# Neighbour counts in two levels, a sort that looks one round ahead, and one addition moved to VectorE in a four-layer graph kernel

## The chip, the cores and the metric

The kernel runs on one core of a Trainium2 chip. The metric is the device time of one execution in microseconds (us): the median of three runs before the change is 5041.57 us (5023.24 to 5044.63). TensorE is called PE, VectorE DVE, ScalarE ACT and GpSimd POOL, as in the profile; SP is the queue that issues plain transfers.

## What is computed

There are 16 independent graphs ("entries") of N = 1024 nodes with C = 64 features. Four layers follow one another, each as `x = layernorm(x + layer(x))`. Layers 0 and 1 multiply the dense 1024 x 1024 adjacency matrix by the features. Layers 2 and 3 first thin out each node's neighbours and then aggregate quantiles over what is left:

```python
nb = (adj_ > 0) & (~eye)
m = nb.sum(-1)
rank = cumsum(nb, axis=-1) - 1
skip = where(m > 10, (m + 1) // 2, 1)
removed = nb & (skip > 1) & mask & ((rank + 1) % skip == 0)
rem = removed | swapaxes(removed, 1, 2)
valid = where(rem, 0, adj_) > 0
# per node and feature: sort the features of the valid neighbours,
# 0.25*q(0.25) + 0.5*q(0.5) + 0.25*q(0.75), interpolated
h = relu((x + agg) @ W1 + b1);  y = h @ W2 + b2
```

With these inputs a node has at most some 33 slots (its own and its neighbours).

## The kernel before

**Tiles and rounds.** The nodes of an entry are ordered by their number of neighbours, so that 128 nodes of like degree stand in one tile. Seven tiles of an entry (10 to 19 slots, `SIZES[:7]`) are filled by POOL: an indirect DMA per slot gathers 128 rows of 64 features from a table in memory (`fetch`, into the ring `got_s` of `ROOM = 60` slots). The eighth tile holds the nodes with the most neighbours; the halves of two entries' eighth tiles are put together to two "end blocks" of 21 and 33 slots (`got`). These are not gathered but picked: VectorE or ScalarE makes a one-hot tile (`hot`) from the slot numbers `place`, and PE multiplies it by the features, split in three bf16 parts (`pick`, 24 matmuls a slot, into `pgk`); ScalarE copies the result out of PSUM (`empty` in `fill`). Only one pair of end blocks is in memory, so that the picks of a round begin when the 33-slot block of the round before is used up.

A round is one layer (2 or 3) of one pair of entries: 8 pairs times 2 layers give 16 rounds. In a round VectorE sorts each tile by a network of min and max operations on slots (`exchange`); ScalarE then multiplies the slots that quantiles need by weights, and PE adds them up by matmuls with an identity (`weigh`); an MLP and a layer norm follow (`finish_round`). In round 0 the two entries' tiles are sorted one by one, later both at once.

**The stages before a round.** For each entry `features` computes layers 0 and 1, `cuts` finds where neighbours are removed, `lists` builds the index lists (takes, pv, keys, order, pk, best, idx) and `ordered` the tables and `place`. `cuts` needs the running count of neighbours up to each column. For each of the eight column tiles t and each half h of 512 columns it adds up, over all row tiles c that come before or within the half, `near` (0 or 1, the stationary operand) times a slice of `steps`, a matrix of ones and zeros with a step: 4 + 8 matmuls of 512 columns a tile, 96 an entry, into `pr`. ScalarE passes over each `pr` twice (Sign with a sum, written to `junk`); the sums tell the columns at which neighbours are cut.

**What sets the order.** Nothing is scheduled by hand, and nothing is decided on the chip. While the program is built, a planner with clocks of its own (`Clocks`, `Weave`) runs all stages as generators, and each instruction is issued when the planner believes that its operands are ready. The order so found is fixed in each engine's queue (VectorE, ScalarE and PE are scheduled by the planner). On the chip each engine takes its instructions in this order and waits where the planner was wrong.

`sorting` calls `sort_round(k)` for one round after the other: it opens `fill(k)`, takes the ring's tiles of this round as they arrive, and an end block when it is filled (an end block that is ready goes ahead of a tile that is ready). When the tiles of the round are done and an end block is not filled, it yields until it is. `allowed[0] = k + 4` lets the stages of later entries begin when round k begins.

In the profile nearly all lines are L300, that of the helper which records each instruction; the tiles' names tell them apart.

Of the kernel before, what the change touches and what calls it, by code (L numbers as in the profile page):

```python
# [22 lines left out]
P = 128  # L23
# [301 lines left out]
def adj_resnorm_kernel(ctx: ExitStack, tc: tile.TileContext, x, adj_t, nodemask, w01, b01, w02, b02,  # L325
# [33 lines left out]

    ONSET = HALF - P  # L360
    steps = const.tile([P, ONSET + N], BF, name="steps")
    row_id = const.tile([P, NT], F32, name="row_id")
    nc.gpsimd.iota(row_id, pattern=[[P, NT]], base=0, channel_multiplier=1,
                   allow_small_or_imprecise_dtypes=True)
# [281 lines left out]
    def cuts(b, e):  # L646

        while e.near is None or (b and not entries[b - 1].taken):
            yield
        near = e.near  # L650

        e.st = st = s.work.tile([P, 6, NT], F32, name="nb_st", bufs=2)
        half = s.work.tile([P, NT], I32, name="nb_half", bufs=1)
        m, dil, lim, cut_at = st[:, 0], st[:, 1], st[:, 2:4], st[:, 4:6]
        mask = mask_all[:, b, :]
        bank, pm = yield from big("pm")
        for t in range(NT):
            for c in range(NT):
                nc.tensor.matmul(pm[:, t : t + 1], near[:, c, t * P : (t + 1) * P], one, start=c == 0, stop=c == NT - 1)
        yield  # L660
        nc.scalar.copy(m, pm[:, :NT])
        read_big[bank] = True
        yield
        dve.tensor_scalar(dil, m, T_THRESH, None, op0=ALU.is_gt)
        dve.tensor_mul(dil, dil, mask)
        dve.tensor_scalar(half, m, 1.0, None, op0=ALU.add)
        dve.tensor_scalar(half, half, 1, None, op0=ALU.logical_shift_right)
        dve.tensor_copy(m, half)
        for i in range(2):
            dve.tensor_scalar(lim[:, i], m, float(i + 1), -NEVER, op0=ALU.mult, op1=ALU.add)  # L670
            dve.tensor_mul(lim[:, i], lim[:, i], dil)
            dve.tensor_scalar(lim[:, i], lim[:, i], NEVER - 0.5, None, op0=ALU.add)
        prs = []
        for t in range(NT + 1):
            if t:
                bank, pr = prs[t - 1]
                for i in range(2):
                    nc.scalar.activation(no_output([P, N]), pr, AF.Sign, bias=lim[:, i, t - 1 : t], scale=-1.0,
                                         accum_out=cut_at[:, i, t - 1 : t], saturate=False)
                read_big[bank] = True  # L680
            if t < NT:
                bank, pr = yield from big("pr")
                prs.append((bank, pr))
                for h in range(NH):
# [12 lines left out]
        e.cut = True  # L697

    def lists(b, e):
# [75 lines left out]
        minus_at = s.work.tile([1, N], F16, name="minus_at", bufs=1)  # L775
# [276 lines left out]
    def weigh(k, t, got, agg, which, present):  # L1052

        want = wants[t]
        while any(e.wts is None for m, b, e in members(k)[1] if m in present):
            yield
        if t >= LISTED:
            wts = members(k)[1][0][2].ends
            for i, slot_id in enumerate(want):
                nc.scalar.activation(got[:, i, :], got[:, slot_id, :], AF.Copy, scale=wts[:, t - LISTED, i : i + 1])  # L1060
                if i % 12 == 11:
                    yield
        else:
            for i, slot_id in enumerate(want):
                for m, b, e in members(k)[1]:
                    if m in present:
                        nc.scalar.activation(got[:, m, i, :], got[:, m, slot_id, :], AF.Copy,
                                             scale=e.wts[:, t, i : i + 1])
                if i % 6 == 5:
                    yield  # L1070
        yield
        prods = got[:, None, : len(want)] if t >= LISTED else got[:, which, : len(want)]
        left = len(want)
        for _ in range(HALVINGS):
            more = left // 2
            dve.tensor_add(prods[:, :, :more], prods[:, :, :more], prods[:, :, left - more : left])
            left -= more
        if HALVINGS:
            yield
        while adding:  # L1080
            yield
        adding.add(k)
        layer, both = members(k)
        for m, b, e in both:
            if m not in present:
                continue
            rows, at = slice(0, P), min(t, NT - 1)
            if t >= LISTED:
                rows, prods = (lower, upper)[halves_of(m).index(t)], got
            else:  # L1090
                prods = got[:, m]
            own = slice(m * C, (m + 1) * C)
            for i in range(left):
                nc.tensor.matmul(acc[own, rows], prods[:, i, :], ident[:, rows], start=i == 0, stop=False)
            nc.tensor.matmul(acc[own, rows], e.xs[layer][:, at, :], ident[:, rows], start=False, stop=True)
        free.add((k, t, present))
        free.add((k, t))
        yield
        if t >= LISTED:
            for m in range(2):  # L1100
                own, rows = slice(m * C, (m + 1) * C), (lower, upper)[halves_of(m).index(t)]
                nc.scalar.copy(agg[own, at, rows], acc[own, rows])
        else:
            own = slice(present[0] * C, (present[-1] + 1) * C)
            nc.scalar.copy(agg[own, at, :], acc[own])
        adding.remove(k)
# [186 lines left out]
    def sort_round(k):  # L1293

        if k >= 2:
            while weave.runs(rounds[k - 2]):
                yield
        weave.add(fill(k))
        agg = s.feat.tile([2 * C, NT, P], F32, name="agg")
        sums = []  # L1300
        todo = [n for n in range(len(tasks)) if tasks[n][0] == k]
        ends = [NS - 2, NS - 1]
        while todo or ends:
            options = []
            if todo and all(fetched[m] > todo[0] for m in tasks[todo[0]][2]):
                got, present = gots[todo[0]], tasks[todo[0]][2]
                options.append((max(clocks.now, clocks.when(got[:, present[0] : present[-1] + 1])), 1, todo[0]))
            if ends and (k, (1, SIZES[NS - 2])[ends[0] - NS + 2]) in filled:
                options.append((max(clocks.now, clocks.when(tails[k][ends[0] - LISTED])), 0, ends[0]))
            if not options:  # L1310
                yield
                continue
            at, is_tile, n = min(options)
# [6 lines left out]
            if is_tile:  # L1320
                _, t, present = tasks[n]
                todo.pop(0)
                got, which, count = gots[n], slice(present[0], present[-1] + 1), len(present)
                other = other[:, : count * SIZES[t], :].rearrange("p (e s) c -> p e s c", e=count)
                yield from exchange(t, (got[:, which], other), cut_pair)
            else:
                t, got, which, present = n, tails[k][n - LISTED], None, (0, 1)
                ends.pop(0)
                yield from exchange(t, (got, other[:, : SIZES[t], :]), cut)
            sums.append(weave.add(weigh(k, t, got, agg, which, present)))  # L1330
        if k:
            while weave.runs(rounds[k - 1]):
                yield
        rounds.append(weave.add(finish_round(k, agg, sums)))

    def sorting():

        for k in range(len(order_of_rounds)):
            allowed[0] = k + 4
            yield from sort_round(k)  # L1340

    with ExitStack() as main:

# [307 lines left out]
```

## Time and profile before

| what | us |
|---|---|
| median of three runs | 5041.57 |
| the profiled execution | 5036.86 |
| its span, first to last instruction | 5035.1 |
| first gather starts / last gather ends | 179.4 / 4961 |
| mean granted clock of PE | 0.85 of full |
| picks: `pgk<-x0p,hot` and `pgk<-x1p,hot`, 24576 matmuls, busy | 976.7 |
| slot weights on ScalarE, `got_s<-got_s,wts`, busy | 398.9 |
| Sign passes `junk<-pr`, 256 of 1111 ns, busy | 284.3 |
| `minus_at<-at_row`, 16 copies of 1 x 1024 on ScalarE, mean | 1.01 |

A group's busy time is what its instructions took together, and the idle time behind the bar is that of the engine just before them, with what ended it. Neighbouring matmuls overlap, so that their spacing is less than their duration. Of pr 1448 of 1536 matmuls are in the trace. Round k's gathers are the k-th 184 in order (2944 in all): those of round 4 begin at 1540 us, those of round 9 at 2963 us, those of round 15 at 4684 us.

### The profile page before, as it was taken

The numbers are of one execution on the slowest core, as the hardware profiler recorded it, in microseconds if no ns is written. First come the engines' busy times: TensorE is split into PE (matmuls) and PEld (weight loads), VectorE is DVE, ScalarE is ACT, GpSimd is POOL, SyncE is SP. The second block draws the span as 40 slices with busy tenths as digits, with TensorE's granted clock in tenths as the row PEclk, the third lists the DMA queues.
The fourth block names the chain that finished last, engine by engine and source line by source line (L and its number), as shares of the span: only waits on it lengthen the run. The fifth ranks groups of instructions, "written<-read, shape, count | busy, mean of one in ns | idle before, by whom it ended". The sixth has DMA issues, their size and how long they took to land. (4 is left out here: it accounts for less than half of the span.)

```text
span 5035.1 us, 123964 instructions
## 1 busy us (share of the span) xinstructions
PE 3791.2 (75%) x50028; PEld 3000.9 (60%) x50200; DVE 4018.0 (80%) x8678; ACT 3079.9 (61%) x7175; POOL 3312.4 (66%) x3168
## 2 busy tenths in 40 slices
PE   6887988887888787888788777888878675563532
PEld 5565666757675665666567575666666554453431
DVE  2568558897898978888888987988798888879593
ACT  4667666657677766667676676666766664452422
POOL 0436217776377775777667675777757776777774
PEclk9989987898999888889899888888988887776765
DMA  3222222322221221222222231222212111111110
GB/s 89 66 68 59 59 65 63 79 58 57 55 67 38 60 64 37 53 68 59 49 55 63 47 72 38 44 68 55 64 46 51 23 30 23 25 30 23 26 24 16
DMA packets 416740, 256.08 MB, mean 51 GB/s; under 512 B 104586, under 2 KB 367002, under 8 KB 416154
## 3 DMA queue, kind: packets, MB, share of 16 engines
q0 software_dynamic: 98304, 100.86, 11.2%
q1 hardware_dynamic: 317850, 147.19, 10.2%
q8 instruction: 395, 6.47, 0.6%
q14 instruction: 191, 1.56, 0.1%
HBM read 235.24 MB, written 12.59 MB: 49 GB/s over the span
## 5 line engine op out<-in xcount | busy, mean ns | idle before, releaser
L300 POOL DMA_INDIRECT got_s<-table,idx x2944 | 3165.2, 1075 | 1629.4 <-issue 509.9
L300 PEld LDWEIGHTS <-hot 128*128 128x128 bf16 x24576 | 902.5, 106 | 457.8 <-issue 265.7
L300 DVE TENSOR_TENSOR other<-got_s 128x512 f32<-128x512 f32 (+9 forms) x850 | 507.0, 609 | 114.6 <-DMA got_s<-table,idx 97.0
L300 PE MATMUL pgk<-x1p,hot 128*128 128x64 bf16 x12288 | 488.7, 205 | 142.0 <-ACT got L300 76.0
L300 PE MATMUL pgk<-ident,got_s 128*64 128x128 f32 x3136 | 423.5, 311 | 226.8 <-ACT got_s L300 177.3
L300 ACT ACTIVATE got_s<-got_s,wts 128x64 f32<-128x64 f32 x1568 | 398.9, 335 | 312.0 <-DVE got_s L300 307.3
L300 PE MATMUL pgk<-x0p,hot 128*128 128x64 bf16 x12288 | 488.0, 204 | 111.9 <-ACT got L300 75.8
L300 PEld LDWEIGHTS pgk<-ident,got_s 128*64 128x64 f32 x3136 | 377.4, 156 | 262.5 <-ACT got_s L300 197.0
L300 PEld LDWEIGHTS <-order 128*128 128x128 bf16 x6912 | 349.2, 100 | 258.6 <-issue 96.4
L300 PEld LDWEIGHTS <-near 128*128 128x128 fp8e4 x4608 | 343.9, 101 | 212.6 <-issue 59.4
L300 DVE TENSOR_SCALAR hot<-place 128x1024 bf16<-128x1024 f16 x768 | 304.1, 437 | 207.3 <-PE pgk L300 195.1
L300 PE MATMUL pk<-near,order 128*128 128x512 fp8e4 x1792 | 438.7, 389 | 0.0
L300 ACT COPY got<-pgk 64x192 f32<-64x192 f32 (+1 forms) x576 | 175.0, 304 | 379.1 <-PE pgk L300 372.6
L300 DVE TENSOR_TENSOR got_s<-other 128x512 f32<-128x512 f32 (+9 forms) x731 | 400.6, 563 | 7.8
L300 DVE TENSOR_TENSOR got_s<-got_s 128x512 f32<-128x512 f32 (+10 forms) x629 | 371.8, 595 | 16.2
L300 PE MATMUL pr<-steps,near 128*128 128x512 bf16 x1448 | 350.9, 386 | 21.3 <-ACT code L300 10.6
L300 ACT ACTIVATE code<-pk,ends_of 128x1024 f16<-128x1024 f32 x224 | 240.0, 1105 | 200.5 <-DVE best L300 101.5
L300 DVE TENSOR_TENSOR other<-other 128x384 f32<-128x384 f32 (+10 forms) x617 | 324.0, 525 | 18.6
L300 ACT ACTIVATE junk<-pr,nb_st 128x1024 fp8e4<-128x1024 f32 x256 | 284.3, 1111 | 62.9 <-PE pr L300 57.3
L300 ACT ACTIVATE hot<-place,minus_k 128x1024 bf16<-128x1024 f16 x256 | 292.7, 1143 | 42.6 <-PE pgk L300 36.4
L300 DVE MAX8 best<-code 128x8 f16<-128x1024 f16 x240 | 283.2, 1216 | 30.1 <-ACT code L300 29.2
L300 ACT ACTIVATE hot<-hot,one_f 128x1024 bf16<-128x1024 bf16 x256 | 294.0, 1148 | 8.4
(200 smaller groups left out, 7122.0 us busy)
## 6 DMA issues: line engine op xcount, KB each, us to landing
adj_r<-in_adj_dram SPq DMA_DIRECT2D x256, 512.0 KB
got_s<-table,idx POOLq DMA_INDIRECT x2944
x_s<-in_x_dram SPq DMA_DIRECT2D x16, 256.0 KB
table<-x2s SPq DMA_DIRECT2D x16, 256.0 KB
table<-xn SPq DMA_DIRECT2D x16, 256.0 KB
out_dram<-xn,out_rows POOLq DMA_INDIRECT x128
table<-no_row SPq DMA_DIRECT2D x12, 0.2 KB
w21s<-in_L_gnn_W_dram SPq DMA_DIRECT2D x2, 32.0 KB
```

Source lines behind the costliest of these rows:

```text
L300: return call(*args, **kwargs)
```

## The change

There are three parts.

1. Counts in two levels. A new constant `after` (zeros, then ones) gives, by 14 matmuls of 512 columns an entry, the number of neighbours in all row tiles before each row tile: `before`, 8 x 1024. ScalarE copies it to `ahead`. Then each half of `pr` begins with one matmul of 512 columns that spreads these eight numbers over the row tiles' columns (by a slice of the identity, broadcast), and each row tile adds its own running count by one matmul of 128 columns. `minus_at`, which `lists` uses, lives in the same constant tile `aside` as `ahead`, in other partitions.
2. `sort_round` and `sorting` become one generator that can have two rounds open. When a round has no ring tiles left, the next is opened (its `fill` queued, its stages allowed), and its tiles are sorted if no end block of the present round is ready. A ready end block still goes first, then tiles of the present round, then those of the next. End blocks of the next round wait.
3. In `weigh`, for rounds 0 and 1, the weighted slots are added in pairs once on VectorE, so that PE has about half of them to add. Before, `HALVINGS = 0` left this out in all rounds.

```diff
+    after = const.tile([P, 2 * NT - 1], BF, name="after")
+    nc.vector.memset(after[:, :NT], 0.0)
+    nc.vector.memset(after[:, NT:], 1.0)
+    aside = const.tile([P // 4 + NT, N], F16, name="aside")
+    minus_at, ahead = aside[:1], aside[P // 4 :]
...
+        bank, po = yield from big("before")
+        blocks = slice(P // 4, P // 4 + NT)
+        for h in range(NH):
+            wide = slice(h * HALF, (h + 1) * HALF)
+            for c in range(NT - 1):
+                nc.tensor.matmul(po[blocks, wide], after[:, NT - 1 - c :][:, :NT], near[:, c, wide], start=c == 0,
+                                 stop=c == NT - 2)
+        yield
+        nc.scalar.copy(ahead, po[blocks])
+        read_big[bank] = True
+        yield
...
                 for h in range(NH):
-                    cs = range((h + 1) * HALF // P)
-                    for c in cs:
-                        nc.tensor.matmul(pr[:, h * HALF : (h + 1) * HALF], near[:, c, t * P : (t + 1) * P],
-                                         steps[:, ONSET + h * HALF - c * P :][:, :HALF], start=c == 0, stop=c == cs[-1])
+                    own = ident_b[blocks, P // 4 + h * G :][:, :G]
+                    nc.tensor.matmul(pr[:, h * HALF : (h + 1) * HALF], ahead[:, rows],
+                                     own[:, :, None].to_broadcast([NT, G, P]), start=True, stop=False)
+                    for c in range(h * G, (h + 1) * G):
+                        nc.tensor.matmul(pr[:, c * P : (c + 1) * P], near[:, c, rows], steps[:, ONSET : ONSET + P],
+                                         start=False, stop=c == (h + 1) * G - 1)
...
-        for _ in range(HALVINGS):
+        for _ in range(1 if k < 2 else 0):
             more = left // 2
             dve.tensor_add(prods[:, :, :more], prods[:, :, :more], prods[:, :, left - more : left])
             left -= more
-        if HALVINGS:
+        if k < 2:
             yield
...
+        while True:
+            if not begun or (len(begun) == 1 and not begun[0].todo):
+                k = begun[-1].k + 1 if begun else len(rounds)
+                if k <= last and (k < 2 or (len(rounds) > k - 2 and not weave.runs(rounds[k - 2]))):
+                    allowed[0] = k + 4
+                    begun.append(open_round(k))
             options = []
-            if todo and all(fetched[m] > todo[0] for m in tasks[todo[0]][2]):
...
+            for later, r in enumerate(begun):
+                if r.todo and all(fetched[m] > r.todo[0] for m in tasks[r.todo[0]][2]):
+                    got, present = gots[r.todo[0]], tasks[r.todo[0]][2]
+                    options.append((max(clocks.now, clocks.when(got[:, present[0] : present[-1] + 1])), 2 * later + 1, r.todo[0], r))
+                if r.ends and not later and (r.k, (1, SIZES[NS - 2])[r.ends[0] - NS + 2]) in filled:
+                    options.append((max(clocks.now, clocks.when(tails[r.k][r.ends[0] - LISTED])), 0, r.ends[0], r))
...
+            if not r.todo and not r.ends:
+                begun.remove(r)
+                while rounds and weave.runs(rounds[-1]):
+                    yield
+                rounds.append(weave.add(finish_round(r.k, r.agg, r.sums)))
+                if r.k == last:
+                    return
```

More of the change, by code (lines that the diff above doesn't have):

```diff
@@ L683, in cuts @@
                 prs.append((bank, pr))
+                rows = slice(t * P, (t + 1) * P)
                 for h in range(NH):
-                    cs = range((h + 1) * HALF // P)
-                    for c in cs:
-                        nc.tensor.matmul(pr[:, h * HALF : (h + 1) * HALF], near[:, c, t * P : (t + 1) * P],
-                                         steps[:, ONSET + h * HALF - c * P :][:, :HALF], start=c == 0, stop=c == cs[-1])
+                    own = ident_b[blocks, P // 4 + h * G :][:, :G]
[4 more added lines that the diff above has]
+                                         start=False, stop=c == (h + 1) * G - 1)
             yield
@@ L774, in lists @@
         yield
-        minus_at = s.work.tile([1, N], F16, name="minus_at", bufs=1)
         nc.scalar.activation(minus_at, pn[:1], AF.Copy, scale=-0.5 / N)
@@ L1291, in exchange, with open_round, sorting @@
             yield clocks.now
[L1293 to L1297, printed above, removed]
+    def open_round(k):
         weave.add(fill(k))
         agg = s.feat.tile([2 * C, NT, P], F32, name="agg")
[L1300 to L1303, printed above, removed]
-            options = []
-            if todo and all(fetched[m] > todo[0] for m in tasks[todo[0]][2]):
[L1306 to L1309, printed above, removed]
+        return SimpleNamespace(k=k, agg=agg, sums=[], todo=[n for n in range(len(tasks)) if tasks[n][0] == k],
+                               ends=[NS - 2, NS - 1])
+    def sorting():
+        last = len(order_of_rounds) - 1
+        begun, sums = [], []
+        while True:
[4 more added lines that the diff above has]
+                    begun.append(open_round(k))
+            options = []
+            for later, r in enumerate(begun):
[4 more added lines that the diff above has]
+                    options.append((max(clocks.now, clocks.when(tails[r.k][r.ends[0] - LISTED])), 0, r.ends[0], r))
             if not options:
@@ L1312, in sort_round @@
                 continue
[L1313 removed]
+            at, rank, n, r = min(options, key=lambda o: o[:3])
             if at > clocks.now:
@@ L1319, in sort_round @@
             other = s.lists.tile([P, WIDE, C], F32, name="other", bufs=1)
-            if is_tile:
+            if rank:
                 _, t, present = tasks[n]
-                todo.pop(0)
+                r.todo.pop(0)
                 got, which, count = gots[n], slice(present[0], present[-1] + 1), len(present)
@@ L1326, in sort_round @@
             else:
-                t, got, which, present = n, tails[k][n - LISTED], None, (0, 1)
-                ends.pop(0)
+                t, got, which, present = n, tails[r.k][n - LISTED], None, (0, 1)
+                r.ends.pop(0)
                 yield from exchange(t, (got, other[:, : SIZES[t], :]), cut)
[L1330 to L1340, printed above, removed]
+            sums.append(weave.add(weigh(r.k, t, got, r.agg, which, present)))
+            r.sums.append(sums[-1])
+            if not r.todo and not r.ends:
[5 more added lines that the diff above has]
+                    return
     with ExitStack() as main:
```

## The prediction

> **What bounds the kernel now.** I read the page's busy line and slices first, then the gathers of POOL in order of time, then the places where POOL stands still, and last the engines in those places.
>
> ```profile
> PE 3791.2 (75%) x50028; PEld 3000.9 (60%) x50200; DVE 4018.0 (80%) x8678; ACT 3079.9 (61%) x7175; POOL 3312.4 (66%) x3168
> ...
> DVE  2568558897898978888888987988798888879593
> ...
> POOL 0436217776377775777667675777757776777774
> ```
>
> No engine is full, so a chain of hand-overs sets the time. POOL is nearer its limit than 66% says. It issues 2944 gathers, and between two that follow at once stand 0.30 us; the group of gathers, by shape, has 1075 ns each:
>
> ```profile
> L300 POOL DMA_INDIRECT got_s<-table,idx x2944 | 3165.2, 1075 | 1629.4 <-issue 509.9 <-DMA got_s<-table,idx 219.7 <-DVE other L300 179.8
> L300 PE MATMUL pr<-steps,near 128*128 128x512 bf16 x1448 | 350.9, 386 | 21.3 <-ACT code L300 10.6 <-ACT junk L300 5.0 <-issue 1.4
> ```
>
> So 2944 x 1.375 = 4048 us of the 5035.1 us span is gathering. The first gather starts at 179 us, the last ends at 4961 us, and 74 us follow. Real standstills of POOL (over 1 us) between these two sum to 569 us in its timeline. Up to 1341 us they are 351 us, mostly waits for an entry's index list or table; after it they are 218 us, about one a round: the ring of 60 slots is full because the sort on VectorE is behind. One of each kind, from the timeline of POOL:
>
> ```profile
> 580.25 0.97 POOL L300 DMA_INDIRECT got_s<-table,idx  x1 [91.82 <-DMA table<-x2s]
> ...
> 739.56 0.94 POOL L300 DMA_INDIRECT got_s<-table,idx  x1 [99.65 <-DVE idx L300]
> ...
> 3127.44 1.84 POOL L300 DMA_INDIRECT got_s<-table,idx  x1 [34.12 <-DVE own L300]
> ...
> 3705.33 1.67 POOL L300 DMA_INDIRECT got_s<-table,idx  x1 [46.24 <-DVE other L300]
> ```
>
> Those 569 us are the ceiling of any gain that leaves the gathers alone. In rounds 3 to 11 VectorE is what fills the ring: it is busy 2386 of the 2780 us from 1340 to 4120. Where does it idle? Between a round's two end blocks. These are four such stretches (rounds 7, 8, 10, 11: from the last operation on the 21-slot block to the first on the 33-slot block), in the table of busy times by stretch, columns PE, weight load, DVE, ACT, POOL:
>
> ```profile
> 2748.30:2776.80 28.50, 24.43 (x403) 16.90 (x405) 3.31 (x12) 19.74 (x40) 21.57 (x23) 1.00 0.15 28
> 3042.30:3065.40 23.10, 22.06 (x360) 16.45 (x362) 3.44 (x7) 13.55 (x31) 17.51 (x18) 1.00 0.15 27
> 3619.50:3643.50 24.00, 23.28 (x386) 17.40 (x390) 5.74 (x12) 17.20 (x38) 18.21 (x20) 1.00 0.20 38
> 3914.50:3936.20 21.70, 20.18 (x303) 13.65 (x306) 2.02 (x4) 15.83 (x35) 16.52 (x18) 1.00 0.17 29
> ```
>
> VectorE works 14.5 of 97.3 us, PE 90. In PE's timeline of the first stretch the picks that fill the end block share PE with the neighbour counts (pr) of a later entry:
>
> ```profile
> 2758.26 2.75 PE L300 MATMUL pr<-steps,near 128*128 128x512 bf16 x11
> ...
> 2762.01 0.87 PE L300 MATMUL pgk<-x0p,hot 128*128 128x64 bf16 x24
> 2762.72 2.75 PE L300 MATMUL pr<-steps,near 128*128 128x512 bf16 x11
> ...
> 2769.51 2.75 PE L300 MATMUL pr<-steps,near 128*128 128x512 bf16 x11
> ```
>
> Four pr blocks, some 10.5 us, lie in those 28.5 us. So between the end blocks PE is the bound, VectorE waits for it with the next round's tiles already gathered, and POOL pays when the ring fills.
>
> **What the Trainium skill says.** "Perfetto Trace Analysis", section "Identifying the Most-Contended Engine": busy time of matmuls is no good measure of PE. The trace agrees: a pr matmul lasts 386 ns, yet the next starts 216 ns later (median). I cost PE by start-to-start spacing. "TensorE: Matmul & The Clock Gate", section "Back-to-back issue gap": N/2.4 + 2.5 ns when warm, 216 ns at 512 columns and 56 at 128, but about 81 ns at 128 columns with a weight load each. Here 128-column matmuls with a load each (there_o) start 56 ns apart, so I use 56. "Perfetto Trace Analysis", section "Identifying Performance Opportunities" ("Consistent bubbles"): a gap that repeats can mean too little room for the next tile; POOL's one gap a round is that. "TensorE: Matmul & The Clock Gate", section "Architectural detail": PE may pull weight loads forward, matmuls stay in order. No run here tests it, but it is why a matmul that waits for ScalarE holds up the picks behind it.
>
> **Counts in two levels.** For an entry, 96 pr matmuls of 512 columns go: 96 x 0.216 = 20.7 us. In come 14 matmuls of 512 columns (before; near as moving operand, which in pk also has 216 ns): 3.0 us; 16 of 512 columns from the copied counts: 3.5 us; 64 of 128 columns at 0.056: 3.6 us. Together 10.1 us, so 10.6 us an entry and 170 us of PE in 16 entries. A pr block of one t falls from 12 x 0.216 = 2.6 to 2 x 0.216 + 8 x 0.056 = 0.9 us. ScalarE gets 16 copies of 8 x 1024; the nearest row (minus_at, 1 x 1024) has 1.01 us, so 16 us; the order of ScalarE's instructions has 16 table loads fewer (48 are in the trace, 1.28 us each), so 20 us go, and ScalarE is even.
>
> What of that is on the path? (i) At the start. Walking back the releasers from the gather at 739.6 us I find 47 us of pr on the chain. Its share 10.6/20.7 would be 24 us, but the block then runs into ScalarE's two passes over each t (2 x (1.11 + 0.19) = 2.6 us, unchanged), and each entry gets the first level, the copy and two hand-overs (3.0 + 1.0 + about 0.3) in front: some 9 us in two entries that are on the chain. I take 15 us. (ii) In rounds 3 to 11, some three pr blocks a round stand in the stretch between the end blocks, 3 x 1.7 = 5 us each: 45 us in nine rounds. The rest of the 170 us is hidden, as PE idles elsewhere (its spacings sum to about 2870 us); it counts only if PE's lateness at other hand-overs matters.
>
> The added wait is that of the first weight load of the copied counts, for ScalarE. Behind it on PE stand picks, behind these ScalarE's evacuations and VectorE's hot tiles. If ScalarE is on time it costs 0.3 us; if ScalarE is itself held by a sort it could be the 25 us that its wait for got_s reaches at most. Below nothing isn't possible. I take 1 us net, in the 5 us above.
>
> **The sort takes the next round's tiles.** The instruction order of the built programs shows how much sorting of ring tiles stands between a round's end blocks on VectorE, at the mean duration of each operation. In round 3 it rises from 34 to 69 us, in 4 from 0 to 21, in 7 and 8 from 0 to 23, in 10 from 0 to 10; in 5, 6, 9 and 11 it doesn't change (in the order the end block counts as filled by then). The idle there was about 9, 14, 25, 19 and 18 us, so up to 9 + 14 + 23 + 19 + 10 = 75 us is covered. What is moved there is missing later, where it covered other waits; I take 45 us. It adds no work. It lets the next entry's loads begin earlier (two 512 KB loads ahead, DMA engines 22% busy): nothing. What is late next is POOL itself: 184 gathers x 1.375 = 253 us a round, plus 11 us for the 8 output scatters of each of the two entries in every second round.
>
> **Adding slots on VectorE in rounds 0 and 1.** 25 adds come: 12 of 192 elements, 6 of 2 x 192 and some to 640, 11.5 us by the rows of those sizes (0.35, 0.56, 0.82). PE loses 140 fp32 matmuls: 88 x 0.11 + 52 x 0.06 = 13 us. VectorE's idle time covers the adds (busy 415 of the first 740 us); without that cover they cost 11.5. PE is on the chain: I take a gain of 5 us, with bounds of +11 and -13.
>
> Sum: -15 - 45 - 45 - 5 = -110 us against the profiled execution (5036.9 us, span 5035.1), which lies 4.7 us under the median 5041.6. Against the median: about 4930 us.
>
> **Rivals.** (A) PE's lateness counts at all hand-overs, and the ring hardly fills any more. For: VectorE's largest waits are for PE (hot 195 us, y_x 72, place 62, y_m 59). Against: POOL's own pace. It would take 180 of the 218 us and 40 at the start: 4820. (B) Nothing reaches the end: ScalarE's passes hold the count blocks, and the planner had hidden the rest; the sort's moved tiles only shift the same idle time. For: in four of nine rounds the order between the end blocks doesn't change. Only some 15 us are left: 5027. (C) Slower: the weight load that waits for the copy of counts stops PE where it is the bound. ScalarE's queue is held up to 25 us by unfinished sorts; a stall of x costs an entry x - 10.6, so it decides from x = 11 on. At 20 us in half the entries on the path (16 x 9.4 = 150, half of it): 5115. Against: ScalarE is idle 39% of the time, and the copy stands right behind the count in order.
>
> **Numbers.** Forecast 0.50, A 0.21, B 0.14, C 0.15. The forecast's own range is 4880 to 4990 (45 us of moved sort could be 0 or 75, (ii) 0 to 90). To leave out no more than 2 in 10, low reaches A and high goes past B: 4815 to 5055. What can be told from no change begins at 0.5%, below 5016 or above 5067. Faster: forecast, A and a third of B, 0.76; within: the rest of B, 0.09; slower: C, 0.15.
>
> **What would show it.** Right: pr blocks of about 0.9 us; POOL's standstills after 1341 us fall from 218 to some 130, those before by 20; in the stretches between end blocks of rounds 4, 7 and 8 VectorE sorts; span about 4925. Wrong: PE idle in front of the copied counts by over 5 us an entry with ScalarE as the releaser (C); unchanged standstills of POOL (B); almost none (A).

## The result and the profile after

The median after the change is 5004.37 us (5002.84 to 5012.34, five runs) against 5041.57 us before; the ratio is 0.994 with a 95% interval of 0.9919 to 0.9961. The gain is 37 us, a third of the 110 us forecast. In 12 of the 18 experiments every kernel, the one before included, took over 7200 us, with about a thousand of TensorE's instructions at steps of 0.70 or 1.40 us, so that of these only ratios are given and all argument rests on the other six.

The page of the kernel after, parts 1 and 2, and the groups by shape (columns as before):

```profile
span 5001.1 us, 123476 instructions
...
PE 3756.2 (75%) x49888; PEld 3003.9 (60%) x49888; DVE 4027.1 (81%) x8705; ACT 3075.5 (61%) x7175; POOL 3335.9 (67%) x3168
...
PEclk7887887888888898988888888889898897776765
```

```profile
L300 POOL DMA_INDIRECT got_s<-table,idx x2944 | 3186.8, 1082 | 1572.2 <-issue 490.6 <-DMA got_s<-table,idx 231.3 <-PE pk L300 177.5
...
L300 PE MATMUL pr<-steps,near 128*128 128x128 bf16 x1024 | 115.2, 243 | 0.0
...
L300 PE MATMUL pr<-ident_b,aside 8*128 8x512 bf16 x256 | 112.1, 438 | 21.3 <-ACT junk L300 8.9 <-ACT code L300 7.0 <-ACT mf L300 3.3
...
L300 PE MATMUL before<-near,after 128*8 128x512 fp8e4 x224 | 51.2, 380 | 0.0
```

The counts fell from 350.9 us of busy time (with 1448 of 1536 matmuls recorded) to 115.2 + 112.1 + 51.2 = 278.5 us. The gathers took 3186.8 us, 21.6 more than before, for the same work. The line of granted clock is lower at its left end; before it read:

```profile
PEclk9989987898999888889899888888988887776765
```

Where did the time go? I follow POOL's gathers, since they end last. This table is worked out from POOL's timelines: the start of round k is that of the (184k + 1)th gather, and the standstills are those of over 1 us between the first and the last gather, each counted where it begins.

| us | before | after | difference |
|---|---|---|---|
| first gather | 179.4 | 184.0 | +4.6 |
| round 3 starts | 1194.6 | 1251.9 | +57.3 |
| round 4 starts | 1540.3 | 1570.8 | +30.5 |
| last gather ends | 4961.1 | 4927.4 | -33.7 |
| standstills up to 1341 us | 351 | 386 | +35 |
| standstills after 1341 us | 218 | 122 | -96 |
| gathers' own time, rounds 4 to 15 | 2388.0 | 2417.7 | +29.7 |

So the middle of the program did what was forecast (a fall from 218 to some 130 us), the start did the opposite, and the gathers became longer. In POOL's timeline of the kernel after, the waits of the start that answer to those at 580.25 and 739.56 us, and one for the ring that before was 7.6 us:

```profile
604.90 0.94 POOL L300 DMA_INDIRECT got_s<-table,idx  x1 [100.06 <-DVE idx L300]
...
759.51 0.94 POOL L300 DMA_INDIRECT got_s<-table,idx  x1 [94.48 <-PE px L300]
...
850.65 0.94 POOL L300 DMA_INDIRECT got_s<-table,idx  x1 [28.23 <-DVE other L300]
```

Between the end blocks VectorE now sorts. The busy times by stretch (PE, weight load, DVE, ACT, POOL) of the two stretches of rounds 7 and 8:

```profile
2757.30:2797.70 40.40, 35.36 (x534) 29.81 (x534) 31.83 (x55) 21.12 (x40) 31.85 (x29) 0.96 0.35 89
3045.50:3083.80 38.30, 30.64 (x352) 25.83 (x350) 34.42 (x59) 21.72 (x45) 30.68 (x26) 0.89 0.32 85
```

VectorE works 66.3 of 78.7 us there, where it worked 6.8 of 51.6 us in the same two rounds before. In round 4 it is 31.2 of 34.9 us, against 3.8 of 18.7. The stretches with a moved sort are longer; a sort once begun is finished before the end block, though not every longer stretch has one (round 11: 31.6 us with 7.9 of VectorE, 21.7 before).

TensorE's clock at the start is the first suspect. Its timeline in the counts of an early entry, before:

```profile
74.36 1.90 PE L300 MATMUL pa<-x,adj_r 128*128 128x65 f32 x16
76.09 2.75 PE L300 MATMUL pr<-steps,near 128*128 128x512 bf16 x12
78.68 1.90 PE L300 MATMUL pa<-x,adj_r 128*128 128x65 f32 x16
```

and after:

```profile
62.48 0.40 PE L300 MATMUL pr<-steps,near 128*128 128x128 bf16 x4
64.11 0.37 PE L300 MATMUL pr<-ident_b,aside 8*128 8x512 bf16 x1 [1.24 <-ACT junk L300]
64.42 0.50 PE L300 MATMUL pr<-steps,near 128*128 128x128 bf16 x4
64.85 0.60 PE L300 MATMUL pr<-ident_b,aside 8*128 8x512 bf16 x1
65.39 0.61 PE L300 MATMUL pr<-steps,near 128*128 128x128 bf16 x4
69.06 0.58 PE L300 MATMUL pr<-ident_b,aside 8*128 8x512 bf16 x1 [3.07 <-ACT junk L300]
...
74.98 3.62 PE L300 MATMUL pa<-x,adj_r 128*128 128x65 f32 x16
```

The shorter blocks wait for ScalarE's passes, and from 64.4 us on all matmuls take longer: 0.37 becomes 0.60, and 16 aggregation matmuls (`pa`) 3.62 us in place of 1.90. The Trainium skill, "TensorE: Matmul & The Clock Gate", "HAM oscillation — how this bites in real kernels", warns of idle gaps of over some 3.4 us that halve the clock. The trace agrees that the clock falls by half, but it fell after a gap of 1.24 us between small matmuls. Nor does the gap decide alone. Before, the clock fell too, at 67.5 us after a gap of 1.98 us, and was back 3.5 us later; after, it stayed at half from 64.6 to some 109 us, although TensorE was busy for 30.03 of the 31 us from 75 to 106. In the busy times by stretch, PE alone (window, length, busy, granted clock, DMA share, GB/s), before:

```profile
60.00:90.00 30.00, 26.98 (x149) 0.94 0.18 53
...
67.50:71.00 3.50, 3.28 (x8) 0.51 0.00 0
71.00:90.00 19.00, 18.17 (x116) 1.00 0.28 84
...
185.00:300.00 115.00, 92.08 (x1036) 0.88 0.27 63
```

and after:

```profile
60.00:90.00 30.00, 23.88 (x123) 0.58 0.12 36
...
75.00:106.00 31.00, 30.03 (x142) 0.50 0.33 98
...
185.00:300.00 115.00, 94.61 (x1002) 0.75 0.29 68
```

### The profile page after: what moved, and what is told of

It reads as the page before. It is cut to its first block, busy times and chain, and to the rows that moved or that the text cites. A ratio compares the mean times of both kernels' runs of the same rounds, so it can differ in the third digit from the quotient of the medians.

```text
span 5001.1 us, 123476 instructions
## 1 busy us (share of the span) xinstructions
PE 3756.2 (75%) x49888; PEld 3003.9 (60%) x49888; DVE 4027.1 (81%) x8705; ACT 3075.5 (61%) x7175; POOL 3335.9 (67%) x3168
## 5 line engine op out<-in xcount | busy, mean ns | idle before, releaser
L300 POOL DMA_INDIRECT got_s<-table,idx x2944 | 3186.8, 1082 | 1572.2 <-issue 490.6
L300 PEld LDWEIGHTS <-hot 128*128 128x128 bf16 x24576 | 934.1, 107 | 490.1 <-issue 268.6
L300 PE MATMUL pgk<-x0p,hot 128*128 128x64 bf16 x12288 | 519.4, 209 | 109.3 <-ACT got L300 71.9
L300 PE MATMUL pgk<-x1p,hot 128*128 128x64 bf16 x12288 | 488.3, 204 | 148.7 <-ACT got L300 78.7
L300 PE MATMUL pgk<-ident,got_s 128*64 128x128 f32 x2960 | 401.9, 311 | 223.9 <-ACT got_s L300 188.1
L300 PEld LDWEIGHTS pgk<-ident,got_s 128*64 128x64 f32 x2960 | 353.4, 156 | 261.9 <-ACT got_s L300 210.1
L300 DVE TENSOR_TENSOR got_s<-got_s 128x512 f32<-128x512 f32 (+9 forms) x650 | 381.4, 590 | 26.5 <-ACT got_s L300 10.4
L300 DVE TENSOR_TENSOR other<-other 128x128 f32<-128x128 f32 (+10 forms) x617 | 323.7, 525 | 18.4
L300 PEld LDWEIGHTS <-near 128*128 128x128 fp8e4 x4096 | 260.1, 102 | 105.0 <-issue 104.1
L300 PE MATMUL pa<-x,adj_r 128*128 128x65 f32 x2048 | 307.3, 314 | 12.8 <-issue 10.7
L300 PEld LDWEIGHTS pa<-x,adj_r 128*128 128x128 f32 x2048 | 298.4, 230 | 24.9 <-issue 16.4
```

The costliest lines, as they stand in the source:

```text
L300: return call(*args, **kwargs)
```

## The experiments

The kernels and the times of the six runs on which the argument rests; the positions are from one profile of each, in us (that of e6 is its fastest run, 4997.8 us):

| run | what | median | ratio to before (95%) | round 3 | round 4 | last gather | standstills to / after 1341 | gathers |
|---|---|---|---|---|---|---|---|---|
| | before | 5041.57 | | 1194.6 | 1540.3 | 4961.1 | 351 / 218 | 3165 |
| | the change | 5004.37 | 0.994 (0.9919 to 0.9961) | 1251.9 | 1570.8 | 4927.4 | 386 / 122 | 3187 |
| e5 | counts alone | 5029.48 | 0.998 (0.9971 to 0.9989) | 1257.1 | 1565.9 | 4949.7 | 360 / 155 | 3195 |
| e6 | change, TensorE kept busy | 5011.74 | 0.9949 (0.9936 to 0.9962) | 1246.7 | 1565.6 | 4922.2 | 381 / 121 | 3190 |
| e13 | sort ahead, old counts in entries 0 to 5 | 5012.0 | 0.9951 (0.9935 to 0.9967) | 1199.6 | 1555.4 | 4942.2 | 359 / 171 | 3187 |
| e15 | sort ahead alone | 5020.39 | 0.9955 (0.9941 to 0.9969) | 1200.7 | 1550.6 | 4950.3 | 359 / 179 | 3184 |
| e16 | counts alone, plan told the old price | 5091.02 | 1.0107 (1.009 to 1.0124) | 1271.7 | 1558.4 | 5013.1 | 340 / 261 | 3173 |
| e17 | the change, old counts in entries 0 to 5 | 4964.71 | 0.9849 (0.9835 to 0.9862) | 1223.9 | 1509.0 | 4892.8 | 289 / 179 | 3199 |

**The counts alone (e5).** The kernel before, with the first part of the diff and nothing else.

> The kernel before with the two-level counts alone, once more, since in the first four runs TensorE began some 1300 of its instructions at steps of 0.70 or 1.40 us and every kernel took over 7200 us. If TensorE runs here as in the profile of before (time of before near 5040 us): theory 1, the clock: the granted clock of 60 to 90 us near 0.6, round 3 starts 30 to 60 us later than 1194.6 us, standstills of POOL after 1341 us near 218 us, time 5060 to 5100 us. Theory 2, the order: round 3 starts at 1175 to 1200 us, time 4990 to 5030 us.

The granted clock of 60 to 90 us was 0.55 and round 3 began 62.5 us late: the two-level counts by themselves make the start late. But the time was 5029 us, under what theory 1 expected and within theory 2's bounds, and the standstills after 1341 us fell from 218 to 155 us. Neither theory holds whole: the start went as theory 1 says, the rest did not.

**TensorE kept busy (e6).** The changed kernel with matmuls that add zeros and that the plan does not see, so that every engine keeps the order of the change:

```diff
+                    for c in range(5 if b < 4 else 0):
+                        whole.tensor.matmul(pr[:, h * HALF : h * HALF + ONSET], near[:, c, rows], steps[:, :ONSET],
+                                            start=False, stop=False)
```

> The changed kernel with the 10 zero-adding matmuls in each block of counts of the first four entries, once more, for the same reason. Theory 1, the clock: granted clock of 60 to 90 us above 0.85, round 3 starts before 1225 us (1251.9 us in the change), time 4960 to 4990 us. Theory 2, the order: round 3 starts at 1255 to 1290 us, time 5005 to 5045 us.

The same table of stretches, e6:

```profile
60.00:90.00 30.00, 27.39 (x199) 1.00 0.12 36
...
185.00:300.00 115.00, 93.96 (x1099) 0.88 0.28 65
```

The clock is back at 1.00 and 0.88, and round 3 began only 5 us earlier. As stated, with the clock as the whole cause, theory 1 falls. Theory 2 has the time right and expected a later round 3 than came. The run does not clear the clock, though: to hold it up, 320 matmuls at some 0.16 us each went in, about 51 us in four entries. Up to the wait for entry 3's list TensorE was busy 619 us here and 620 us in the change, so that the zeros took what the clock gave back. In e6 the clock also stayed at 1.00 over a gap of 1.64 us.

**Old counts in the first entries (e13, e17).** In e13 the sort reaches ahead, slots are added as before, and the two-level counts are used from entry 6 on; e17 has the slots on VectorE too, so that it differs from the change by this alone (the same condition stands around the first level):

```diff
-                for h in range(NH):
+                if b >= 6:
...
+                else:
...
```

> The sort that takes the next round's tiles, with the old counts in entries 0 to 5 and the two-level counts in entries 6 to 15, slots added as before; alone in its call, since in e7 to e12 TensorE again began a thousand of its instructions at steps of 0.70 or 1.40 us. If before runs near 5040 us: theory 3, the start is late because of the two-level counts in the first entries (their plan and their lower clock): round 3 at 1185 to 1210 us, the later rounds have the change's relief of TensorE, 4930 to 4965 us, faster than either kernel. Theory 4, any new plan loses the luck of the old one: round 3 at 1215 us or later, 4980 to 5020 us.

The start came back: round 3 at 1199.6 us. The second half of theory 3's expectation did not: 5012 us, since the rounds from 4 on gained 34 us (3386.8 in place of 3420.8) and not the change's 64.

> The whole change, but with the old counts in entries 0 to 5: that is e13 with slots added on VectorE in rounds 0 and 1. Theory 3: the start is that of before and the rest that of the change, since nothing else was lost: round 3 at 1185 to 1215 us, rounds 4 to 15 as long as in the change (3356 to 3380 us), time 4970 to 4995 us, faster than the change. Theory 8, what is lost at the start is handed back anyway (the change's round 3 is 27 us shorter than before's), and the slots are worth little: rounds 3 to 15 as in e13 (some 3740 us from round 3 to the last gather), time 5005 to 5020 us.

4964.7 us: 1.5% faster than before and, by the medians, 40 us faster than the change. By the bounds written down, round 3 was 9 us outside theory 3's and the later rounds 4 us (3383.8 us from round 4 on), while the time is 5 us better. The clock of the start is that of before:

```profile
60.00:90.00 30.00, 25.69 (x151) 1.00 0.19 55
...
185.00:300.00 115.00, 89.81 (x1036) 0.87 0.26 65
```

What moved is to be read in round 4: 1509.0 us, against 1570.8 in the change. The wait of POOL for entry 3's list is longer than before's 99.65 us, and the standstills of 21.7, 17.7 and 31.0 us that before had between 1257 and 1341 us are gone:

```profile
767.28 0.94 POOL L300 DMA_INDIRECT got_s<-table,idx  x1 [129.67 <-PE pk L300]
```

So the 40 us belong to the two-level counts of the first six entries, together with the plan that comes with them. Less e13, e17 also says that the slots are worth 47 us here. At the start of round 1 they give 7.5 us (571.7 against 579.2), as forecast; at the starts of rounds 2 and 3 e17 is 19.3 and 24.3 us behind e13, and by round 4 it is 46 us ahead, as those three standstills (70 us) are gone and the wait for entry 3's list is 31 us longer (98.6 us in e13).

**Price and work (e16).** Is it the plan, which believes that the counts are cheap? The counts of e5, while the plan is charged what the old blocks cost:

```diff
+                clocks.on = False
...
+                clocks.on = True
+                for h in range(NH):
+                    for c in range((h + 1) * HALF // P):
+                        clocks.put("PE", "matmul", (pr[...], near[:, c, rows], steps[...]), {})
```

> The kernel before with the two-level counts, while the plan is charged each block of counts at its old price (12 matmuls of 512 columns on average), so that it orders the engines' programs nearly as before; as e9, in a call without e14's kernel. Theory 3a, the plan: the start is late because the plan, told of cheap counts, puts other work ahead; then round 3 is back at 1185 to 1215 us (1257.1 us with the counts alone) and the time at 4985 to 5015 us. Theory 3b, the work: TensorE's saving at the start is taken back by its lower clock (each block of 16 aggregation matmuls 3.6 us in place of 1.9) and by ScalarE's passes, whatever the order; then the lists of entry 3 are later than 750 us (739.6 us before), round 3 at 1225 to 1265 us, and the time 5020 to 5040 us.

Entry 3's list came at 798 us, round 3 at 1271.7 us, and the whole was 1% slower than before. That excludes 3a as stated: with the old price the start stays late. It goes with 3b at the start, though round 3 is 7 us past 3b's bound, and 5091 us is far above it: a plan that is told of a busier TensorE than there is loses another 61 us against e5. Nor is the order of before restored by the old price: by entry 3's list TensorE had done 2016 pick matmuls of `x0p` in e16 and in e5, against 1536 before and in the change. But e17 has 2016 there too and is the fastest, so that this place in the order is not what decides.

**The sort alone (e15).** The second part of the diff and nothing else (and 16 matmuls that add zeros in the last entry).

> The sort that takes the next round's tiles alone, as in e14, with 16 further matmuls that add zeros in the counts of the last entry (under 3 us of TensorE, which shift the instructions behind them and nothing else). Every call with e14's kernel has so far met the state in which TensorE begins a thousand of its instructions at steps of 0.70 or 1.40 us, and no call without it has. If before runs near 5040 us: theory 6, the sort that reaches ahead is worth what was forecast: round 3 within 12 us of 1194.6 us, POOL's standstills of over 1 us in rounds 4 to 15 fall from 368 us to 310 to 330 us, time 4985 to 5005 us. Theory 7, it moves VectorE's work into time in which VectorE was not what POOL waited for: the standstills of those rounds stay within 20 us of 368 us, time 5025 to 5045 us.

Round 3 was 6 us late and the standstills after 1341 us fell from 218 to 179 us. For rounds 4 to 15 that is from 368 to 333 us (here with the output scatters, which lie between gathers), against an upper bound of 330 for theory 6 and a lower one of 348 for theory 7: closer to 6, while the time, 5020 us, lies between both. The missing 19 us are in the gathers: 3184 in place of 3165 us.

**The other twelve runs.** Ratios, each to before beside it:

| what | ratios |
|---|---|
| counts alone (e1) | 0.9861 |
| sort ahead alone (e2, e7, e11, e14) | 0.9777, 0.9777, 0.9777, 0.9761 |
| slots alone (e3, e8, e18) | 0.995, 0.9986, 0.9953 |
| change, TensorE kept busy (e4) | 0.9836 |
| counts, old price (e9) | 1.0145 |
| sort ahead, old counts in entries 0 to 5 (e10, e12) | 0.9864, 0.9851 |

What was expected of them was written for a time of before near 5040 us, so that its numbers in us couldn't be met or missed. The first four were to set theory 1, the clock, against theory 2, the order:

> The kernel before with the two-level counts alone. Theory 1, the clock: the blocks of counts now end before ScalarE has passed over the last one, TensorE stands between them, its granted clock falls over the first entries and the start runs late. Then the window 60 to 90 us has a granted clock near 0.6 (0.94 before), the first gather of round 3 comes 30 to 60 us later than the 1194.6 us of before, the standstills of POOL after 1341 us stay near 218 us, and the time is 5060 to 5100 us. Theory 2, the order: the start of the change is late because the sort that reaches ahead and the longer adding on VectorE have displaced the work of the entries; then the counts alone are harmless at the start, round 3 is at 1175 to 1200 us, and the time is 4990 to 5030 us.

> The kernel before with the sort that takes the next round's tiles alone. Theory 1, the clock: nothing is changed before 1194 us that matters; the granted clock of 60 to 90 us stays near 0.94, round 3 starts within 10 us of 1194.6 us, the standstills of POOL after 1341 us fall from 218 us to 130 to 180 us, and the time is 4960 to 5000 us. Theory 2, the order: the start is late here, round 3 at 1220 to 1250 us, with the clock high, and the time is 5010 to 5060 us.

> The kernel before with slots added on VectorE in rounds 0 and 1 alone. Theory 1, the clock: no part in the late start; round 2 within 8 us of the 937.7 us of before, the rest as before, 5025 to 5045 us. Theory 2, the order: VectorE's added work is what makes rounds 1 to 3 late; round 2 starts 10 to 25 us later, and the time is 5050 to 5065 us.

> The changed kernel with 10 further matmuls of 384 columns that add zeros in each block of counts of the first four entries, some 1.6 us of TensorE's time a block, 51 us in all; the instructions of all other engines and their order are as in the change. Theory 1, the clock: TensorE no longer stands between the blocks, the granted clock of 60 to 90 us goes back above 0.85, round 3 starts before 1225 us (1251.9 us in the change), and the time is 4960 to 4990 us. Theory 2, the order: TensorE only has more to do; round 3 starts at 1255 to 1290 us and the time is 5005 to 5045 us.

The next set theory 3, the plan told of cheap counts, against theory 4, that any new plan loses the start (e13 and e15 then settled that, against theory 4):

> The kernel before with the sort that takes the next round's tiles alone, on a chip that runs before near 5040 us. After e5 and e6 the clock no longer explains the late start (with it restored, round 3 still began at 1246.7 us), and the counts alone show it (1257.1 us). Theory 3, the plan: told that the counts are cheap, the plan puts work of rounds 0 and 1 ahead of the entries' lists. Then this kernel, whose counts are old, keeps the start: round 3 within 12 us of 1194.6 us, standstills of POOL after 1341 us 130 to 180 us, time 4960 to 4990 us. Theory 4, any new plan loses the luck of the old one: round 3 here too at 1215 us or later, time 4995 to 5040 us.

> The kernel before with slots added on VectorE in rounds 0 and 1 alone. Theory 3: the start stays within 12 us (round 3 at 1183 to 1207 us), time 5025 to 5045 us. Theory 4: round 3 at 1215 us or later, or earlier than 1175 us, and the time moves by over 0.3% either way.

> The kernel before with the two-level counts, while the plan is charged each block of counts at its old price (12 matmuls of 512 columns on average), so that it orders the engines' programs nearly as before. Theory 3, the plan: round 3 back at 1185 to 1215 us (1257.1 us with the counts alone), time 4985 to 5010 us. Theory 5, the work: the two-level counts themselves cost TensorE as much as they save at the start, since its clock falls and each spread matmul and each aggregation runs slower; then round 3 stays at 1235 to 1265 us and the time at 5020 to 5035 us.

> The sort that takes the next round's tiles, with the old counts in entries 0 to 5 and the two-level counts in entries 6 to 15, slots added as before. Theory 3: the start is that of before (round 3 at 1185 to 1210 us) and the later rounds have the change's relief of TensorE, so 4930 to 4965 us, faster than either kernel. Theory 4: round 3 at 1215 us or later, 4980 to 5020 us.

> The kernel before with the sort that takes the next round's tiles alone, once more, since in e7 to e10 TensorE again began a thousand of its instructions at steps of 0.70 or 1.40 us. If before runs near 5040 us: theory 3, the plan told that the counts are cheap is what makes the start late: round 3 within 12 us of 1194.6 us, standstills of POOL after 1341 us 130 to 180 us, time 4960 to 4990 us. Theory 4, any new plan loses the luck of the old one: round 3 at 1215 us or later, time 4995 to 5040 us.

> The sort that takes the next round's tiles, with the old counts in entries 0 to 5 and the two-level counts in entries 6 to 15, slots added as before; once more, for the same reason. Theory 3: round 3 at 1185 to 1210 us and the later rounds have the change's relief of TensorE, so 4930 to 4965 us, faster than either kernel. Theory 4: round 3 at 1215 us or later, 4980 to 5020 us.

The last two asked what the sort and the slots are worth alone; the first of these was answered by e15:

> The kernel before with the sort that takes the next round's tiles alone. e13 has put the late start on the two-level counts of the first entries, and its rounds from 4 on gained 34 us where the change gained 64. If before runs near 5040 us: theory 6, the sort that reaches ahead is worth what was forecast: round 3 within 12 us of 1194.6 us, POOL's standstills of over 1 us in rounds 4 to 15 fall from 368 us to 310 to 330 us, time 4985 to 5005 us. Theory 7, it moves VectorE's work only into time in which VectorE was not what POOL waited for: the standstills of those rounds stay within 20 us of 368 us, time 5025 to 5045 us.

> The kernel before with slots added on VectorE in rounds 0 and 1 alone; as e3 and e8, in a call without e14's kernel. e17 with the slots is 47 us faster than e13 without them, where 5 us were forecast. Theory 9, the slots are worth that by themselves, since TensorE's additions of slots stand in the way of the lists of the first entries: round 4 starts at 1490 to 1520 us (1540.3 us before), time 4990 to 5015 us. Theory 10, they are worth it only with the other parts, through the order that the plan then finds: round 4 at 1530 us or later, time 5025 to 5050 us.

In us none of these can be compared with anything above, and the slots alone have no other runs: what they are worth by themselves stays open. That the counts with the old price are slower than before shows in both groups of runs (1.0107 in e16, 1.0145 in e9).

## Why the prediction was wrong

Against the profile before, 110 us were forecast: 20 at the start (15 and the slots' 5) and 90 from round 3 on. The last gather ended 33.7 us earlier. Of the 76 us that are missing, 50 were lost before round 4 (+30.5 in place of -20) and 26 after it (-64 in place of -90); the split is rough, since a part of the 90 was forecast for round 3.

**The start: the step "I take 15 us" failed.** It had the sign wrong; the start lost 30.5 us at round 4. One term under it was mis-sized, and one was missing.
- A block of one t was to take 2 x 0.216 + 8 x 0.056 = 0.9 us. It takes 1.20 us at full clock (median of 126 in the trace after) and up to 1.96 at the lower one (90th percentile). The 128-column matmuls do follow one another at 0.056 us, but the matmul after a spread one begins 0.317 us after it, not 0.216, and a spread one begins 0.151 us after a 128-column one, not 0.056. The first level (3.0 forecast, 3.19 measured) and ScalarE's copy (1.0, 1.00) were right.
- The trace before showed this price. In `pk` a matmul with a stationary operand of 1 x 128 stands ahead of those of 128 x 128, and the next begins 0.317 us after it (median of 224); in `pv`, where operands and column counts change but the stationary operand stays 128 x 128, the spacing is 0.216 us at 512 columns and 0.056 at 128. I priced the 8 x 128 operand by the wrong neighbours:

```profile
105.94 0.38 PE L300 MATMUL pv<-takes,minus_i 128*128 128x512 bf16 x1
106.16 0.22 PE L300 MATMUL pv<-ident_b,near 128*128 128x128 bf16 x1
...
151.09 0.39 PE L300 MATMUL pk<-minus_at,steps 1*128 1x512 f16 x1
151.41 1.90 PE L300 MATMUL pk<-near,order 128*128 128x512 fp8e4 x8
```

- So the 10.6 us an entry were not there. Up to entry 3's list the pr work of four entries took 87.7 us of TensorE before (364 of 384 matmuls recorded, so some 92) and 27.9 + 27.5 + 12.5 = 67.9 us after: 5 to 6 us an entry.
- Missing was the clock. In the same stretch `pa`, which the change doesn't touch, went from 65.8 to 86.5 us, and the 20 us saved were gone; in e6, with the clock held up, it took 57.9. In all TensorE was busy for 608 us up to that list before and for 620 after. I saw that the block "runs into ScalarE's two passes" and drew from it only that the gain is cut, not that TensorE, made to wait, runs its other work slower.
- In all eight kernels of the table TensorE is idle for 128 to 139 us of the time up to entry 3's list, while it is busy for 608 (before) to 674 us (e5): the list is late by about as much as TensorE has more to do ahead of it. That is not all of the start, for e17's list comes at 767.3 us and its round 4 is the earliest.
- These terms take the gain away; they do not add up to the loss of 30.5 us. How much of the late start is this work and how much is order stays open. e13 and e17 show that it belongs to the two-level counts of the first entries, e16 that charging the old price does not bring the start back, e6 that holding up the clock at a cost of 51 us doesn't pay. A kernel with exactly before's order and the new matmuls was not tried.

**Relief between the end blocks and the sort ahead: right in mechanism.** 45 + 45 us were forecast. The standstills after 1341 us fell by 96 us in the change, by 39 with the sort alone and by 63 with the counts alone. VectorE sorts where it was said to, in rounds 4, 7 and 8. The counts alone (e5) shorten the stretches of rounds 8, 10 and 11 from 23.1, 24.0 and 21.7 us to 15.9, 17.2 and 11.6, where 5 us each were forecast.

**What is late next: a term was missing.** "What is late next is POOL itself: 184 gathers x 1.375" took the gather's time as fixed. It is not: of the 94 us of standstill that left rounds 4 to 15, 30 came back as longer gathers. The gathers, sorted by the share of their time in which VectorE works:

| rounds 4 to 15 | under 10% | 10 to 90% | over 90% |
|---|---|---|---|
| before: gathers, mean us | 197, 0.944 | 282, 1.000 | 1729, 1.111 |
| after: gathers, mean us | 156, 0.944 | 271, 1.011 | 1781, 1.121 |

Closing VectorE's gaps moves gathers from the first column to the last, which is worth 8 of the 30 us; the other 22 are longer gathers within the columns, and why they are longer stays open. It is also not any work of VectorE that counts. Before, the 65 gathers that lay beside `max8` alone (128 x 1024, 1.22 us) took 0.943 us, as beside an idle VectorE; the 24 beside `tensor_tensor` alone of 128 x 1024 (1.22 us too) took 1.34 us, and the 84 beside 128 x 512 took 1.10. The Trainium skill, "SBUF — State Buffer", "SBUF: two separate sides", says that VectorE and GpSimd share a pair of ports, which VectorE takes in some operations only, those with two inputs in SBUF among them (against a GpSimd operation that reads SBUF), and that the other engine then waits until the instruction ends. The trace agrees in that the operation decides; that the ports are the cause was not tested.

**Slots: forecast -5, bounds +11 and -13.** e17 less e13 gives -7.5 us at round 1, +19 and +24 at rounds 2 and 3, -46 at round 4 and -47 in the whole: only the first is within the bounds. The plan's order changes with the slots, and I had no term for that; that the order is what is worth this much was not shown by itself.

**The rivals.** C, the wait for the copied counts, did not come: TensorE waited 4.5 us for `aside` in the whole program. A did not come. B had the start half right (ScalarE's passes hold the blocks) and the rest wrong (the sort did not only shift idle time), yet 5004 us lies nearer to its 5027 than to the forecast's 4930 and outside the forecast's own 4880 to 4990. The wide range, 4815 to 5055, held the time; that is no merit of the mechanism at the start.

## What to carry to other kernels

A matmul block that is shortened until another engine sets its pace saves nothing there, and may slow its neighbours through the clock. Here the longer block in the first entries and the shorter one later, where TensorE is the bound, did better (e17: -1.5%, the change -0.6%). Price a new matmul with a small stationary operand by one in the trace whose operand is small too. Time an engine's instruction beside busy neighbours and beside idle ones, and by what they do, before counting it as fixed. Where a planner fixes the order, every edit is also a new order: judge the parts one by one, and at several places of the trace, since a late start can be half repaid by the next round.

## What was not expected of the hardware

- A stationary operand of another size costs spacing: the next matmul begins 0.317 us after one of 512 columns with 8 x 128 (`pr` after) or 1 x 128 (`pk`, before and after), and the 8 x 128 one 0.151 us after one of 128 columns, against 0.216 and 0.056 us where the operand stays 128 x 128.
- The granted clock fell from 0.94 to 0.58 in 60 to 90 us: it fell after a gap of only 1.24 us, in a stretch of 8-row and 128-column matmuls, and stayed at half although TensorE was busy for 30.03 of the 31 us from 75 to 106. With 384-column matmuls of zeros in the blocks it was 1.00. What decides is open.
- An indirect gather's issue on GpSimd takes 0.944 us beside an idle VectorE or beside `max8`, and 1.34 us beside a `tensor_tensor` of 128 x 1024.
